# Writing two masked operands of a state-space scan over all 128 partitions

## The chip, the cores and the metric

The kernel runs on one core of one Trainium2 chip. The metric is the device time of one execution in microseconds (us), given as the median of several runs. A single profiled execution supplies the page and the trace from which the other numbers come. Its engines are called PE (TensorE, matrix products), DVE (VectorE), ACT (ScalarE), POOL (GpSimd) and SP (SyncE, which here only issues transfers).

## The reference

The reference is one block of a network on `x` of shape (4, 512, 256): four batch rows, 512 positions, 256 channels. It computes a modulated layer norm, a state-space attention (32 heads, head dimension 8, state size 64) added with a gate, a second modulated layer norm and a gated feed-forward layer with a Walsh-Hadamard transform, added with another gate. The part that matters here is the attention:

```python
xBC, z, A_log = jnp.split(proj, [CONV_DIM, CONV_DIM + D_INNER], axis=-1)
xc = lax.conv_general_dilated(xBC.transpose(0, 2, 1), conv_w, (1,), [(D_CONV - 1, 0)], ...)
x, Bm, Cm = jnp.split(xBC, [D_INNER, D_INNER + NH * D_STATE], axis=-1)
...
a = -jax.nn.softplus(A_log).transpose(0, 2, 1)
Lm = jnp.exp(segsum(a))
M = jnp.einsum('blhn,bshn,bhls->bhls', Cm, Bm, Lm)
y = jnp.einsum('bhls,bshp->blhp', M, x)
y = y + D[None, None, :, None] * x
out = (y * jax.nn.silu(z + z_bias)) @ W_out.T
```

Every head has a lower-triangular 512 x 512 matrix of decays, and `x` of that head (512 x 8) is multiplied by it.

## The kernel before, in words

The sequence is cut into 8 chunks of 64 positions (`Q`, `NC`). Within a chunk the kernel uses the quadratic form (`attend`, `intra`). Between chunks it carries states: `states` sums decayed `B` times `x` over each chunk, `turn_states` transposes those sums and runs a scan over the chunks on DVE, and `inter` multiplies `C` by the result.

The work is split in units `n = (i, b)`: half `i` of the heads (16 of them) and batch row `b`, eight in all. A unit has 8 steps `k`, one for each pair of heads (one partition half for each head of the pair). A step projects `B` and `C` with six PE matrix products each (`project`, `proj`, L242), applies a causal convolution of width 4 to each (`conv`: two ACT operations, two DVE operations at L378 and L379, one POOL operation at L380), transposes `B` (`turn_b`) and forms the masked products with the decays (`attend`; DVE at L446). Four steps make a group `m`; its parity is `pp`. `states`, `intra`, `turn_states` and `inter` run once for each `m`.

The change concerns `x_part3`, which runs once for each unit, and what it feeds. After the convolution of `x` (`x_proj`), `x_part2` makes two copies of each chunk side by side, so that a PE transpose of 128 columns yields the 64 positions of a chunk twice: on partitions 0 to 63 and again on 64 to 127. There are two such halves of a unit (`hf`), of four chunks each, and the transposed tile `pt` of a half is [128, 4 chunks, 128 channels] in PSUM. From it DVE makes two operands in SBUF:

- `xpad`, the weights of `intra`: for each `pp`, chunk and group `g`, 32 columns, of which the head of the lower partition half has its 8 columns filled on partitions 0 to 63 and the head of the upper half on 64 to 127. All else is zero, written once at the start by a POOL memset (L149). Four copies a half unit fill it (L506).
- `xwz`, the weights of `states`: `x` times the decay to the end of its chunk (`wdec`), with the even chunk of a pair on the lower partitions and the odd one on the upper, each in its own 16 of 32 columns, and zeros elsewhere from the same memset. Four products a half unit fill it (L514).

`wdec` is made once for each batch row in part 4 of `prologue`, by one ACT copy of a PE transpose (L366). `own` is a constant of ones and zeros loaded at the start. `own[p, 0, c]` is 1 where the partition half of `p` equals the half `c // 8` of the 16 columns; `turn_states` uses the whole of it to mask the states.

The order of work is set in two layers. The kernel pushes calls on an agenda with due times (`at_time`, and the table `T`), measured in steps `k`, and the program is traced in that order; unit `n`'s `x_part3` is due at 8n + 3.77, just ahead of `states` of its first group. A planner then orders the instructions on each engine when the program is built, by its own estimate of when each is ready, and gives the tiles their places in SBUF and PSUM. SP's transfers alone keep the order of tracing. PSUM tiles of the tag `m` (transposes, `pG`, `pl`, state sums, `pw`) share three buffers, and the projections (tag `p`) share three more.

After step 64 the kernel goes over to the feed-forward stage (`ffn_up`, `ffn_down`), of which the first pieces overlap the last steps of the scan.

Of the kernel before, what the change touches and what calls it, by code (L numbers as in the profile page):

```python
# [13 lines left out]
F32 = mybir.dt.float32  # L14
F32R = mybir.dt.float32r
BF16 = mybir.dt.bfloat16
AF = mybir.ActivationFunctionType
ALU = mybir.AluOpType
# [4 lines left out]
NH, HD = 32, 8  # L23
# [7 lines left out]
def mamba_ffn(tc, ctx, u, c_t, wmod, win_t, cw, cb, zb, dsk, wo_t, w13_t, w2_t,  # L31
              k_ident, k_reset, k_dl, k_dr, k_had, k_own, out):
    nc = tc.nc
    ve, ac, gp, pe = nc.vector, nc.scalar, nc.gpsimd, nc.tensor
# [4 lines left out]
    const = E(tc.tile_pool(name="const", bufs=1))  # L39
# [15 lines left out]
    def cload(src, shape, name, eng=nc.scalar):  # L55
        t = const.tile(shape, F32, name=name)
        eng.dma_start(t, src)
        return t
# [10 lines left out]
    def load_x(which, b, src, step=4):  # L69
        t = work([128, 4, DM], f"x{which}{b}", "x", 1)  # L70
        for n in range(0, 4, step):
            nc.sync.dma_start(t[:, n : n + step], src[:, n : n + step])
        return t

    def tok_rows(ap):
        return ap.rearrange("(t p) d -> p t d", p=128)
# [25 lines left out]
    ident = cload(k_ident, [128, 128], "ident", nc.sync)  # L102
# [41 lines left out]
    own = cload(k_own, [128, 4, 16], "own")  # L144
    xpad = const.tile([128, 2, NC, 4, 32], F32, name="xpad")
    sts = [const.tile([128, NC - 1, 4, 32], F32, name=f"sts{pp}") for pp in range(2)]
    xwz = const.tile([128, 4, 4, 2, 2, 16], F32, name="xwz")
    for t in (xpad, xwz):
        gp.memset(t, 0.0)  # L149

    dls = [const.tile([94, 8, 128], BF16, name=f"dl{n}") for n in range(2)]
    drs = [const.tile([94, 4, S], BF16, name=f"dr{n}") for n in range(2)]
# [110 lines left out]
    def normalize(b, which, x):  # L263
        mv = work([128, 4, 2], f"mv{which}{b}", "mv")
        rs = work([128, 4], f"rs{which}{b}", "rs")
        xn = work([128, 4, DM], f"xn{which}{b}", "xn", 1)
        for t in range(4):
            bs = work([128, 6], f"bs{which}{b}{t}", "bs")
            ve.bn_stats(bs, x[:, t])
            ve.bn_aggr(mv[:, t], bs)  # L270
        ve.tensor_scalar(rs, mv[:, :, 1], EPS, None, ALU.add)
        last[gp] = gp.tensor_tensor(rs, rs, neghalf, ALU.pow)
        for t in range(4):
            ve.tensor_scalar(xn[:, t], x[:, t], mv[:, t, 0:1], rs[:, t : t + 1], ALU.subtract, ALU.mult)
        return xn
# [19 lines left out]
    def spill(name, tiles):  # L295
        d = dram.tile([128, 2, 2, S], F32, name=name)
        for k in range(2):
            after(2, nc.sync.dma_start, d[:, k], tiles[k].bitcast(F32))
        return d
# [10 lines left out]
    wdec, p_dr, p_dr3, p_end = {}, {}, {}, {}  # L310
# [3 lines left out]
    def prologue(b, part, fill=None):  # L314
        if part == 0:
            if b not in x_in:
                x_in[b] = load_x(0, b, tok_rows(u[b]))
            xns[b] = normalize(b, 0, x_in.pop(b))
        elif part == 1:
            fulls[b], ht[0, b] = modulate(b, 0, xns.pop(b))  # L320
            htd[b] = spill(f"htd{b}", ht[0, b])
        elif part == 2:

            full = fulls.pop(b)
            pa = mtile([128, 128], f"pa{b}")
            for k in range(2):
                for t in range(4):
                    last[pe] = pe.matmul(pa[32 * t : 32 * t + 32], wa[:, k], full[k][:, 128 * t : 128 * t + 128],
                              start=(k == 0), stop=(k == 1), skip_group_check=True, tile_position=(0, 32 * t))
            e = work([128, 128], f"spe{b}", "spe", 1)  # L330
            at = work([128, 128], f"at{b}", "at", 1)
            ac.activation(e, pa, AF.Abs)
            last[ve] = ve.tensor_scalar(at, pa, 0.0, -1.0, ALU.max, ALU.mult)
            if fill:
                fill()
            ac.activation(e, e, AF.Exp, scale=-1.0)
            ac.activation(e, e, AF.Ln, bias=1.0)
            ve.tensor_tensor(at, at, e, ALU.subtract)
            phs = phss[b] = work([128, 128], f"phs{b}", "phs", 1)
            ve.tensor_tensor_scan(phs, reset, at, 0.0, ALU.mult, ALU.add)  # L340

            parts = work([128, 3, 128], f"parts{b}", "parts", 1, BF16)
            rest = work([128, 128], f"rest{b}", "at", 1)
            ve.tensor_copy(parts[:, 0], phs)
            ve.tensor_tensor(rest, phs, parts[:, 0], ALU.subtract)
            ve.tensor_copy(parts[:, 1], rest)
            last[ve] = ve.tensor_tensor(parts[:, 2], rest, parts[:, 1], ALU.subtract)
            p_dr3[b] = dram.tile([NH, 3, S], BF16, name=f"p3{b}")
            p_dr[b] = dram.tile([NH, S], F32, name=f"pd{b}")
            p_end[b] = dram.tile([NH, NC], F32, name=f"pend{b}")  # L350
            for t in range(4):
                (gp if T["p3gp"] and b == 0 and t % 2 else nc.sync).dma_start(p_dr3[b][:, :, 128 * t : 128 * t + 128], parts[32 * t : 32 * t + 32])
            after(1, write_sums, b, phs)
        elif part == 3:

            phs = phss.pop(b)
            df = dfs[b] = work([128, 128], f"df{b}", "df", 1)
            p_c = phs.rearrange("p (c l) -> p c l", l=Q)
            ve.tensor_tensor(df.rearrange("p (c l) -> p c l", l=Q), p_c[:, :, Q - 1 :].to_broadcast([128, 2, Q]),
                             p_c, ALU.subtract)  # L360
            ac.activation(df, df, AF.Exp)
        else:
            pw = mtile([128, 128], f"pw{b}")
            pe.transpose(pw, dfs.pop(b), ident)
            wdec[b] = const.tile([128, 4, NH], F32, name=f"wd{b}")
            ac.activation(wdec[b].rearrange("p t h -> p (t h)"), pw, AF.Copy)  # L366

    def write_sums(b, phs):
        for t in range(4):
# [126 lines left out]
    def x_part3(n):  # L496
        i, b = units[n]
        for hf, xd in enumerate(xds.pop(n)):
            pt = mtile([128, 4, 128], f"xt{n}{hf}")
            for c in range(4):  # L500
                pe.transpose(pt[:, c], xd[:, c].rearrange("p r l -> p (r l)"), ident)
            for pp in range(2):
                for j in range(2):
                    o = 8 * (2 * pp + j)
                    src = pt[64 * j : 64 * j + 64].rearrange("p c (g x) -> p c g x", g=4)[:, :, :, o : o + 8]
                    ve.tensor_copy(xpad[64 * j : 64 * j + 64, pp, 4 * hf : 4 * hf + 4, :, o : o + 8], src)  # L506
            for q in range(2):
                sl = slice(64 * q, 64 * q + 64)
                for t in range(2):
                    tt = 2 * hf + t  # L510
                    src = pt[sl, 2 * t + q].rearrange("p (a h x) -> p a h x", h=2, x=8)
                    dst = xwz[sl, tt, :, :, q].rearrange("p g a (h x) -> p (g a) h x", x=8)
                    wv = wdec[b][sl, tt, 16 * i : 16 * i + 16].rearrange("p (a h) -> p a h", h=2)
                    ve.tensor_tensor(dst, src, wv.unsqueeze(3).to_broadcast([64, 8, 2, 8]), ALU.mult)  # L514

    def states(m):
        pp = m % 2
        pst = mtile([128, 4, 128], f"ps{m}")
        for t in range(4):
            for g in range(4):  # L520
                pe.matmul(pst[32 * g : 32 * g + 32, t], xwz[:, t, g, pp].rearrange("p q x -> p (q x)"),
                          bts[4 * m + g][:, t], start=True, stop=True, tile_position=(0, 32 * g))
        for g in range(4):
            bts.pop(4 * m + g)
        stt[m] = work([128, 4, 128], f"st{m}", "st", 1)
        ac.activation(stt[m], pst, AF.Copy)
# [16 lines left out]
    def turn_states(m):  # L543
        n, pp = divmod(m, 2)
        st = stt.pop(m)
        pt = mtile([128, 4, 16, NC], f"sT{m}")
        for t in range(4):
            pe.transpose(pt[:, :, :, 2 * t : 2 * t + 2].rearrange("p g x q -> p g q x"), st[:, t], ident)
        sn = work([128, 4, 16, NC], f"sn{m}", "xd", 2)
        ve.tensor_tensor_scan(sn.rearrange("p g x c -> p (g x c)"),  # L550
                              dcs[n][:, 8 * pp : 8 * pp + 8].rearrange("p h x c -> p (h x c)"),
                              pt.rearrange("p g x c -> p (g x c)"), 0.0, ALU.mult, ALU.add)
        o = 16 * pp
        gp.tensor_tensor(sts[pp][:, :, :, o : o + 16].rearrange("p c g x -> p g x c"), sn[:, :, :, : NC - 1],
                         own.unsqueeze(3).to_broadcast([128, 4, 16, NC - 1]), ALU.mult)
# [323 lines left out]
```

## Time and profile before

| | us |
|---|---|
| median of 3 runs | 608.14 (607.9 to 608.25) |
| profiled execution, its own time | 611.31 |
| its span, first to last instruction | 609.4 |
| PE busy in the span | 549.5 |
| DVE busy | 454.3 |
| ACT busy | 367.5 |
| POOL busy | 314.9 |

The profiled execution is 3.2 us longer than the median, and 1.9 us of its own time lie outside the span. Its mean granted PE clock was 0.976. In the views that follow, a group is named by line, engine, operation, and output and input tiles; a wait is written "engine line <- engine line that released it: us in total, times, longest". Busy time of an engine is not a sum of durations where neighbours overlap: DVE reports the next operation of a run before the last one has ended.

### The profile page before, as it was taken

The page shows a single profiled execution, that of the slowest core. Times are in us where ns is not written, and L with a number is a line of the kernel's source. Part 1 is how long each engine was busy: PE and PEld are TensorE (multiplying, and loading weights), DVE is VectorE, ACT ScalarE, POOL GpSimd, SP SyncE. Part 2 cuts the span into 40 slices and gives each one's busy share as a digit, 9 for nine tenths or more (in the row PEclk, how much of TensorE's full clock was granted, in tenths as well). Part 3 has the DMA queues.
Part 4 walks back from the last instruction along what each step waited for, and adds up shares of the span by engine and source line. Part 5 has one row for each costly group of instructions (what it writes and reads, how often), then busy time and mean ns, then how long its engine had stood idle before and what let it go on. Part 6 is the DMA issues. An engine that isn't in the chain of part 4 may idle for free. (4 is left out here: it accounts for less than half of the span.)

```text
span 609.4 us, 16345 instructions
## 1 busy us (share of the span) xinstructions
PE 549.5 (90%) x6836; PEld 435.8 (72%) x6836; DVE 454.3 (75%) x820; ACT 367.5 (60%) x600; POOL 314.9 (52%) x288
## 2 busy tenths in 40 slices
PE   3777898899889979999999899979979999999996
PEld 3554676678667756676777576757857888888886
DVE  5978798897796879889879888989888384343342
ACT  5657678867867765697785678567643233322221
POOL 5564243644534476764655558456576545325341
PEclk9978999999889989999999999999988999999999
DMA  6331111020313305201501244145139033304021
GB/s 199 107 127 70 40 37 72 10 67 3 105 27 101 110 2 164 92 3 58 170 4 37 75 131 146 58 131 176 37 119 298 9 124 117 125 0 147 1 78 36
DMA packets 42113, 52.00 MB, mean 85 GB/s; under 512 B 18230, under 2 KB 30260, under 8 KB 42040
## 3 DMA queue, kind: packets, MB, share of 16 engines
q1 hardware_dynamic: 40504, 50.54, 26.2%
q8 instruction: 54, 0.88, 0.6%
q10 hardware_dynamic: 1472, 0.38, 0.3%
q14 instruction: 19, 0.16, 0.1%
q0 software_dynamic: 64, 0.05, 0.0%
HBM read 33.51 MB, written 17.44 MB: 84 GB/s over the span
## 5 line engine op out<-in xcount | busy, mean ns | idle before, releaser
L380 POOL TENSOR_TENSOR cc<-cc,cv 128x509 f32<-128x509 f32 x64 | 70.5, 1101 | 75.2 <-DVE cc L379 69.7
L380 POOL TENSOR_TENSOR bc<-bc,cv 128x509 f32<-128x509 f32 x64 | 71.3, 1114 | 58.0 <-DVE bc L379 34.5
L242 PE MATMUL f<-h,wf 128*128 128x512 f32 x384 | 98.3, 396 | 0.0
L242 PEld LDWEIGHTS f<-h,wf 128*128 128x128 f32 x384 | 69.4, 191 | 12.3
L694 POOL TENSOR_TENSOR fl<-ft,fh 128x512 fp32r<-128x512 f32 x31 | 40.1, 1294 | 64.1 <-ACT fh L693 60.7
L375 ACT ACTIVATE cc<-pcc,cb_sb,cw_sb 128x512 f32<-128x512 f32 x64 | 49.8, 778 | 26.5 <-PE pcc L242 15.0
L375 ACT ACTIVATE bc<-pbc,cb_sb,cw_sb 128x512 f32<-128x512 f32 x64 | 50.0, 781 | 24.7 <-PE pG L255 15.2
L242 PE MATMUL pcc<-ht,wq 128*128 128x512 f32 x192 | 55.7, 428 | 10.0 <-DVE bc L379 8.1
L378 DVE SCALAR_TENSOR_TENSOR cc<-pcc,cw_sb,cc 128x511 f32<-128x511 f32 x64 | 47.4, 741 | 20.9 <-ACT cv L377 19.9
L242 PE MATMUL pbc<-ht,wq 128*128 128x512 f32 x192 | 56.7, 432 | 5.5 <-DVE cc L379 4.0
L693 ACT ACTIVATE fh<-ft 128x512 fp32r<-128x512 f32 x32 | 20.2, 632 | 66.9 <-PE pdyi L701 36.8
L689 DVE SCALAR_TENSOR_TENSOR ft<-ft,f 128x512 f32<-128x512 f32 x32 | 21.9, 687 | 49.6 <-ACT ft L688 45.4
L242 PE MATMUL pcc<-hr,wq 128*128 128x512 f32 x192 | 52.1, 405 | 3.0 <-ACT cv L377 1.5
L242 PE MATMUL pbc<-hr,wq 128*128 128x512 f32 x192 | 51.7, 404 | 2.2 <-DVE cc L379 2.0
L242 PEld LDWEIGHTS pcc<-ht,wq 128*128 128x128 f32 x192 | 37.4, 202 | 20.4 <-DVE bc L379 4.1
L454 ACT ACTIVATE bt<-bT 128x512 f32<-128x512 f32 x64 | 38.6, 604 | 19.6 <-PE bT L452 19.5
L378 DVE SCALAR_TENSOR_TENSOR bc<-pbc,cw_sb,bc 128x511 f32<-128x511 f32 x64 | 47.3, 740 | 3.0 <-ACT cv L377 3.0
L242 PEld LDWEIGHTS pbc<-ht,wq 128*128 128x128 f32 x192 | 37.2, 203 | 17.3 <-DVE cc L379 1.9
L379 DVE SCALAR_TENSOR_TENSOR bc<-pbc,cw_sb,bc 128x510 f32<-128x510 f32 x64 | 47.4, 741 | 1.2
L379 DVE SCALAR_TENSOR_TENSOR cc<-pcc,cw_sb,cc 128x510 f32<-128x510 f32 x64 | 47.4, 741 | 1.1
L452 PE MATMUL bT<-ident,bc 128*128 128x128 f32 x256 | 41.8, 286 | 3.9 <-DVE cc L379 1.2
L377 ACT ACTIVATE cv<-pcc,cw_sb 128x512 f32<-128x512 f32 x64 | 43.7, 683 | 2.0 <-POOL bc L380 2.0
(148 smaller groups left out, 1237.0 us busy)
## 6 DMA issues: line engine op xcount, KB each, us to landing
wq<-win_t SPq DMA_DIRECT2D x16, 256.0 KB
htd<-ht SPq DMA_DIRECT2D x8, 512.0 KB
hr<-htd SPq DMA_DIRECT2D x8, 512.0 KB
h2d<-ht SPq DMA_DIRECT2D x8, 512.0 KB
h<-h2d SPq DMA_DIRECT2D x8, 512.0 KB
x<-u SPq DMA_DIRECT2D x7, 512.0 KB
ex<-pd SPq DMA_DIRECT2D x8, 256.0 KB
ygd<-yg SPq DMA_DIRECT2D x4, 512.0 KB
```

The costliest lines, as they stand in the source:

```text
L242: last[pe] = pe.matmul(ps, w[:, a, k, c0 : c0 + 128], ht[k][:, b], start=(n == 0), stop=(n == 5))
L375: ac.activation(dst, ps, AF.Identity, bias=cb_sb[:, tl : tl + 1], scale=w[:, 3:4])
L377: last[ac] = ac.activation(v, ps, AF.Copy, scale=w[:, 0:1])
L378: ve.scalar_tensor_tensor(dst[:, 1:], ps[:, : S - 1], w[:, 2:3], dst[:, 1:], ALU.mult, ALU.add)
L379: ve.scalar_tensor_tensor(dst[:, 2:], ps[:, : S - 2], w[:, 1:2], dst[:, 2:], ALU.mult, ALU.add)
L380: last[gp] = gp.tensor_tensor(dst[:, 3:], dst[:, 3:], v[:, : S - 3], ALU.add)
L452: pe.transpose(pt[:, t], bc[:, 128 * t : 128 * t + 128], ident)
L454: ac.activation(bts[k], pt, AF.Copy)
L689: ve.scalar_tensor_tensor(t, t, 1.0, p1, ALU.add, ALU.mult)
L693: ac.activation(hi, t, AF.Copy)
L694: (ve if (b, f) == (NB - 1, 7) else gp).tensor_tensor(lo, t, hi.bitcast(F32), ALU.subtract)
```

## The change

All operations that fill `xpad` and `xwz` now cover all 128 partitions, and the zeros come from masks instead of from partition slices and the memset. For `xpad`, one product of a half's `pt` with `own[:, 0]` writes both `pp` and all four groups; the view `v` addresses the 16 columns of each `pp` (0 to 15 and 16 to 31). For `xwz`, `wdec` gets an axis `q` for the even and the odd chunk of a pair, and is written by two ACT copies, each with a column of `own` as its scale, which zeroes the partition half that `q` doesn't own. One product for each pair of chunks then fills `xwz`. The layout of `xwz` goes from (group, pp, q, 16 columns) to (head, q, 8 columns), so `states` takes two heads at a time, and the transposes in `turn_states` write their columns in the order that puts the states back as before. `xwz` needs no memset.

```diff
-    xwz = const.tile([128, 4, 4, 2, 2, 16], F32, name="xwz")
-    for t in (xpad, xwz):
-        gp.memset(t, 0.0)
+    xwz = const.tile([128, 4, 16, 2, 8], F32, name="xwz")
+    gp.memset(xpad, 0.0)
...
-            wdec[b] = const.tile([128, 4, NH], F32, name=f"wd{b}")
-            ac.activation(wdec[b].rearrange("p t h -> p (t h)"), pw, AF.Copy)
+
+            wdec[b] = const.tile([128, 4, 2, NH], F32, name=f"wd{b}")
+            for q in range(2):
+                ac.activation(wdec[b][:, :, q], pw.rearrange("p (t h) -> p t h", h=NH), AF.Copy,
+                              scale=own[:, 0, 8 * q : 8 * q + 1])
...
-            for pp in range(2):
-                for j in range(2):
-                    o = 8 * (2 * pp + j)
-                    src = pt[64 * j : 64 * j + 64].rearrange("p c (g x) -> p c g x", g=4)[:, :, :, o : o + 8]
-                    ve.tensor_copy(xpad[64 * j : 64 * j + 64, pp, 4 * hf : 4 * hf + 4, :, o : o + 8], src)
-            for q in range(2):
-                sl = slice(64 * q, 64 * q + 64)
-                for t in range(2):
-                    tt = 2 * hf + t
-                    src = pt[sl, 2 * t + q].rearrange("p (a h x) -> p a h x", h=2, x=8)
-                    dst = xwz[sl, tt, :, :, q].rearrange("p g a (h x) -> p (g a) h x", x=8)
-                    wv = wdec[b][sl, tt, 16 * i : 16 * i + 16].rearrange("p (a h) -> p a h", h=2)
-                    ve.tensor_tensor(dst, src, wv.unsqueeze(3).to_broadcast([64, 8, 2, 8]), ALU.mult)
+
+            v = xpad[:, :, 4 * hf : 4 * hf + 4, :, :16].rearrange("p a c g x -> p a (c g) x")
+            v = bass.AP(v.tensor, v.offset, [v.ap[0], [v.ap[1][0] + 16, 2], *v.ap[2:]])
+            ve.tensor_tensor(v, pt.rearrange("p c (g a x) -> p a (c g) x", g=4, a=2),
+                             own[:, 0].unsqueeze(1).unsqueeze(1).to_broadcast([128, 2, 16, 16]), ALU.mult)
+            for t in range(2):
+                ve.tensor_tensor(xwz[:, 2 * hf + t].rearrange("p h q x -> p q h x"),
+                                 pt[:, 2 * t : 2 * t + 2].rearrange("p q (h x) -> p q h x", x=8),
+                                 wdec[b][:, 2 * hf + t, :, 16 * i : 16 * i + 16]
+                                 .unsqueeze(3).to_broadcast([128, 2, 16, 8]), ALU.mult)
...
-                pe.matmul(pst[32 * g : 32 * g + 32, t], xwz[:, t, g, pp].rearrange("p q x -> p (q x)"),
+                pe.matmul(pst[32 * g : 32 * g + 32, t], xwz[:, t, 4 * g + 2 * pp : 4 * g + 2 * pp + 2].rearrange("p h q x -> p (h q x)"),
...
-            pe.transpose(pt[:, :, :, 2 * t : 2 * t + 2].rearrange("p g x q -> p g q x"), st[:, t], ident)
+            pe.transpose(pt[:, :, :, 2 * t : 2 * t + 2].rearrange("p g (h x) q -> p (g h) q x", h=2), st[:, t], ident)
```

## The prediction

> **What bounds the kernel now.** I read the busy shares first, then a table by stage, then the places that the change touches, then who waits for whom.
>
> ```profile
> PE 549.5 (90%) x6836; PEld 435.8 (72%) x6836; DVE 454.3 (75%) x820; ACT 367.5 (60%) x600; POOL 314.9 (52%) x288
> ```
>
> The shares alone name TensorE (PE), but they average over stages. A table of busy time over four stretches (us; each engine's busy time with its instruction count, then clock and DMA) separates them:
>
> ```profile
> 0.00:65.00 65.00, 42.63 (x307) 32.08 (x307) 50.85 (x104) 42.97 (x65) 33.54 (x39) 0.92 0.38 120
> 65.00:470.00 405.00, 373.05 (x5698) 285.80 (x5699) 345.47 (x623) 285.52 (x472) 224.87 (x204) 0.98 0.27 84
> 480.00:610.00 130.00, 124.05 (x734) 109.93 (x733) 53.33 (x88) 36.07 (x60) 49.95 (x40) 0.99 0.23 74
> ```
>
> The third column is PE, the fifth is VectorE (DVE). After 480 us, in the feed-forward stage, PE works 124 of 130 us and DVE only 53: nothing that DVE saves counts there. All eight places of the change lie between 65.7 and 440.1 us, in the scan stage. There PE is busy 373.05 of 405 us, so 32 us of PE idle is all that a change off PE can win back, and DVE is busy 345 us (85%). The waits of PE in that stretch say who keeps it idle:
>
> ```profile
> PE sT L548 <- DVE l L446: 7.0, 4, 4.0
> PE pcc L242 <- DVE bc L379: 5.6, 5, 1.9
> PE pbc L242 <- DVE cc L379: 4.9, 4, 1.6
> PE pcc L242 <- ACT cv L377: 3.2, 2, 1.7
> PE ps L521 <- DVE xwz L514: 1.4, 4, 0.4
> ```
>
> Adding up every row of that answer, about 28 us of PE's waits end on DVE and 4 us on ACT. Few are on the tiles of the change itself (1.4 us on `xwz`): DVE is late with convolutions and products that queue behind other DVE work. The eight blocks of `x_part3` are such work. In windows of 8 us around each:
>
> ```profile
> 64.00:72.00 8.00, 6.25 (x115) 4.34 (x113) 7.76 (x22) 4.42 (x9) 2.18 (x2) 1.00 0.16 25
> 118.80:126.80 8.00, 7.46 (x123) 5.27 (x121) 7.73 (x23) 5.17 (x9) 2.89 (x3) 1.00 0.22 49
> 171.50:179.50 8.00, 6.53 (x112) 4.62 (x112) 7.73 (x23) 5.74 (x11) 1.09 (x1) 0.79 0.13 32
> 226.50:234.50 8.00, 7.43 (x122) 5.46 (x120) 7.76 (x23) 4.90 (x9) 3.45 (x3) 1.00 0.64 199
> 274.00:282.00 8.00, 7.20 (x123) 4.94 (x121) 7.73 (x23) 5.74 (x10) 3.16 (x3) 1.00 0.32 109
> 378.30:386.30 8.00, 8.00 (x137) 7.06 (x136) 7.77 (x22) 4.05 (x7) 2.90 (x3) 1.00 0.01 2
> ```
>
> DVE is full in every one (about 7.75 of 8). PE loses 1.75, 0.54, 1.47, 0.57 and 0.80 us in the first five, 5.1 us together, and nothing in the last three. The chain of waits can be followed back only to 328 us, and within it the two complete blocks lie on it from end to end (379.66 to 384.08 and 435.99 to 440.40).
>
> **What the Trainium skill says.** "VectorE: DVE Perf Modes", section "The TRN2 errata", gives (N+151)/0.96 ns for an fp32 product of two tensors of N elements a partition: 291 ns for 128 and 691 for 512, where this trace has 284 (L514) and 680 (L446). The same section says that many small tiles each pay the fixed part, which a large one pays once. Its section "Why PSUM operands drop a tier" lets no fp32 operation that reads PSUM run above one element a cycle, so replacing the PSUM copies by products loses no faster mode; the trace agrees, 287 ns a copy against 284 a product. "SBUF — State Buffer" is the last place: its section "Who interferes with whom" has VectorE and GpSimd share a port, with two-SBUF-input operations affected. The new products read one operand from PSUM, and the rows of that kind hold still here (L446 673 to 692 ns), while L338, with both operands in SBUF, takes 871 ns for 128 elements.
>
> **The change, part by part.**
>
> *Removed from DVE.* Per half unit four 64x128 copies (L506) and four 64x128 products (L514). One block on DVE:
>
> ```profile
> 379.58 1.21 DVE L506 COPY xpad<-xt 64x128 f32<-64x128 f32 x4
> 380.80 0.99 DVE L514 TENSOR_TENSOR xwz<-xt,wd 64x128 f32<-64x128 f32 x4
> 381.83 1.21 DVE L506 COPY xpad<-xt 64x128 f32<-64x128 f32 x4
> 383.05 1.00 DVE L514 TENSOR_TENSOR xwz<-xt,wd 64x128 f32<-64x128 f32 x4
> 384.08 0.75 DVE L379 SCALAR_TENSOR_TENSOR cc<-pcc,cw_sb,cc 128x510 f32<-128x510 f32 x1
> ```
>
> From 379.58 to 384.08 it holds DVE 4.50 us, 2.25 a half, 36.0 us over eight units.
>
> *Added to DVE.* Per half one 128x512 product of PSUM with a broadcast mask, and two of 128x256. For 512, L446 and L604 give 680 ns; a pair of L446 takes 1.28 us, so one step of a run is 0.60. For 256 no row of this kind exists: on the line between 284 (128) and 680 (512) it is 416 ns (424 by the page's formula), and between the steps 0.25 and 0.60 it is 0.37. A half is then 0.60 + 2 x 0.37 = 1.34 us, a unit 2.68: **relief of 1.82 us a unit, 14.6 us in all**. If nothing overlaps, a half is 0.68 + 2 x 0.42 = 1.52, and the relief 1.46 a unit, 11.7 in all. I take 1.82.
>
> *Added to ACT.* `wdec` takes two ACTIVATEs in place of one, four times: 4 x 278 ns (L366) = 1.1 us on an engine that is 60% busy. Its first reader comes at 66.9 us and the first L366 at 34.7; the later ones, up to 177.4, are likewise some 50 us ahead of theirs. The tile `pw` holds one of three shared PSUM buffers 0.28 us longer. I cost this at nothing; with its cover gone, 1.1 us.
>
> *Removed from POOL.* The memset of `xwz`, 952 ns at 2.50. POOL then sits idle 0.83 us until ACT's `th`, and the first PE work waits for a DMA until 8.07: nothing gained.
>
> *Moved in order.* The two layouts of `xwz` give the weights of `states` as 32 contiguous numbers either way. The transposes of `turn_states` write PSUM in runs of 8 instead of 16 at the same stride; L548 (strided, 285 ns) and L452 (dense, 286) cost the same, so I price that at nothing, with 0.1 us a unit on either side. No DMA is moved, and no queue is passed. The first product of a half serves both `pp` at once, so it must wait for the last `intra` of the unit before to have read `xpad`; those reads end some 20 us earlier (355.75 before the block at 379.58): no wait.
>
> *What reaches the end.* In the first five blocks the relief is larger than or about equal to PE's idle time, but part of that idle ends on ACT or on PE's own order: I take 60% of 5.1, **3.1 us**. In the other three PE has no gap; DVE merely comes out 1.8 us ahead, which shows at the next wait of PE on DVE, and PE does the same work in between: a third of 3 x 1.82, **1.8 us**. Sum 4.9 us. What is late next is PE itself and ACT's `cv` (18.4 us of DVE's own waits in the stage). The profiled execution took 611.31 us (span 609.4 and 1.9 around it), 3.2 above the median of the three runs; the gain is a difference, so I take it from the median: 608.14 - 4.9 = 603.2 us.
>
> **The rivals.**
>
> *Hidden.* PE is busy 92% of the stage and gap-free in three of the blocks, so DVE might gain slack that only becomes waiting for PE and ACT (59 us of DVE idle exist in the stage already). Against it: 28 us of PE's waits end on DVE. Time: 607 to 608.5.
>
> *The order shifts, slower.* Instruction order is fixed by a planner at build time, and it does react: at 67.91 us a convolution stands between the halves of the first block, at 381.8 nothing does. New durations, and 2 KB a partition more for `wdec`, may place other work differently. The mechanism with a price: `turn_states` needs one of the three shared PSUM buffers and finds it held by `pG` until DVE makes `l` (L446). That wait occurs four times now, 7.0 us, 1.75 each. Four more would cost 7.0, net of 4.9 a loss of 2.1: 610.2 us. It decides from three additional ones on (4.9/1.75 = 2.8). It is the case that ends on the other side.
>
> *More passes through.* If every block delays PE downstream, most of the relief counts: 8 to 11 us, 597 to 600; the ceiling is 14.6, so 593.5.
>
> *The products are dearer.* With three free dimensions and a doubly repeated operand they might run at half rate: 2 x 1.52 = 3.0 a half, 12 us more DVE work, a third of it on the path, 612 us. L514 already walks three free dimensions with a repeated operand at 284 ns, so this is unlikely, as is a splitting of the operations.
>
> **How the numbers follow.** The forecast (601 to 606.5) 0.45; more passes 0.17; hidden 0.12, of which a third is still over 0.2% faster; the shift 0.22; dearer products 0.04. Under 0.2%, 1.2 us, this kernel can't be told from no change. So faster 0.66, same 0.10, slower 0.24. The range 597 to 611 takes in half of the shift's cases and most of the larger gain; the likeliest case alone is 601 to 606.5.
>
> **What would show it.** In the changed profile: 16 products of `xpad` at 0.68 us and 32 of `xwz` at 0.42; DVE busy down by 11 to 15 us in all; a block of 2.7 us; eight ACTIVATEs of `wd` at 0.28; PE idle between 65 and 470 us down from 32 to about 27, with the FFN stage unchanged. The forecast is wrong if PE's waits on DVE don't fall, or if waits of `sT` on `l` grow.

## The result, and the profile after

The changed kernel takes 603.18 us in the median of 14 runs (599.66 to 606.49), against 608.08 for the kernel before in its 14 (606.44 to 610.71): a ratio of 0.9916, 95% interval 0.9891 to 0.994. It is 4.9 us faster, clear of the bound of 0.2%. The profiled execution took 605.11 us, with a span of 603.2.

The page of the changed kernel, busy time of each engine (share of the span) and instructions:

```profile
PE 544.0 (90%) x6836; PEld 435.3 (72%) x6836; DVE 438.3 (73%) x740; ACT 368.5 (61%) x604; POOL 313.3 (52%) x287
```

DVE has 80 instructions and 16.0 us less. PE keeps its 6836 products. One block on DVE, from its timeline (start, duration, engine, line, operation), now reads:

```profile
375.61 0.68 DVE L507 TENSOR_TENSOR xpad<-xt,own 128x512 f32<-128x512 f32 x1
376.21 0.74 DVE L510 TENSOR_TENSOR xwz<-xt,wd 128x256 f32<-128x256 f32 x2
376.87 0.68 DVE L507 TENSOR_TENSOR xpad<-xt,own 128x512 f32<-128x512 f32 x1
377.47 0.74 DVE L510 TENSOR_TENSOR xwz<-xt,wd 128x256 f32<-128x256 f32 x2
378.13 0.73 DVE L381 SCALAR_TENSOR_TENSOR cc<-pcc,cw_sb,cc 128x510 f32<-128x510 f32 x1
```

From 375.61 to 378.13 it holds DVE 2.52 us, where the old one held it 4.50. The rows by line give the single prices (engine, operation, count, then shortest, median and longest in ns):

```profile
L507 DVE TENSOR_TENSOR xpad<-xt,own x16: 677/679/681, 62.4 to 431.4; 128x512 f32<-128x512 f32 x16
L510 DVE TENSOR_TENSOR xwz<-xt,wd x32: 409/413/416, 63.6 to 432.4; 128x256 f32<-128x256 f32 x32
L367 ACT ACTIVATE wd<-pw,own x8: 361/368/422, 34.7 to 173.0; 128x128 f32<-128x128 f32 x8
```

The two products cost what was forecast. How many partitions take part hardly matters: the straight line through 413 and 679 ns, both on 128 partitions, gives 280 ns for 128 elements, and the old products on 64 partitions took 284. The `wdec` copies are dearer than the plain copy was.

So far all agrees. The waits of PE between 65 and 470 us do not; these are the largest rows (us in total, times, longest):

```profile
PE pbc L241 <- DVE cc L381: 5.2, 5, 1.6
PE pcc L241 <- DVE bc L381: 4.3, 6, 1.8
PE sT L547 <- DVE l L448: 4.2, 3, 1.9
PE ps L520 <- DVE l L448: 2.7, 2, 2.5
PE pt L283 <- DVE sn L549: 2.6, 2, 1.3
PE pl L418 <- DVE sn L549: 2.6, 2, 1.9
PE pbc L241 <- DVE bc L381: 2.5, 1, 2.5
```

All rows together, 27.6 us still end on DVE, and it was 28. `sT` waits less, as do `pcc` and `xwz`; but `ps`, `pt`, `pl` and `pbc` have waits that were smaller before or absent. A gain that leaves the suspected waits as large as they were isn't explained by them. Nor does the pair of profiles show where PE saved its time: the span is 6.2 us shorter, but PE's idle time in it only fell from 59.9 to 59.2 us. The other 5.5 us are busy time of the same 6836 products, at a mean granted clock of 0.976 and 0.980; what shortened it isn't shown. The planner had put many instructions in another order, on PE and DVE above all, so two things changed at once: the work and the order.

### The profile page after: what moved, and what is told of

The parts are those of the page before. It is cut to its first block, busy times and chain, and to the rows that moved or that the text cites. A ratio compares the mean times of both kernels' runs of the same rounds, so it can differ in the third digit from the quotient of the medians.

```text
span 603.2 us, 16262 instructions
## 1 busy us (share of the span) xinstructions
PE 544.0 (90%) x6836; PEld 435.3 (72%) x6836; DVE 438.3 (73%) x740; ACT 368.5 (61%) x604; POOL 313.3 (52%) x287
## 4 chain that ended last, share of the span: by engine, by line
PE 61%; DVE 19%; DMA 8%; ACT 7%; issue 3%; SPq 2%; POOL 1%; ACTq 0%; DVEq 0%; POOLq 0%
PE f L241 14%; PE pcc L241 9%; PE pbc L241 9%; PE pdy L700 4%; PE pdyi L700 4%; PE py L536 3%; PE bT L454 3%; PE pG L254 3%; PE ps L520 3%; DVE cc L380 2%; PE po L600 2%; DMA wq<-win_t 2%; PE pz L241 2%; DVE l L448 2%; DMA x<-u 2%
## 5 line engine op out<-in xcount | busy, mean ns | idle before, releaser
L377 ACT ACTIVATE bc<-pbc,cb_sb,cw_sb 128x512 f32<-128x512 f32 x64 | 49.9, 780 | 35.0 <-PE pG L254 18.4
L377 ACT ACTIVATE cc<-pcc,cb_sb,cw_sb 128x512 f32<-128x512 f32 x64 | 49.8, 778 | 23.2 <-PE pcc L241 13.7
L241 PEld LDWEIGHTS pbc<-hr,wq 128*128 128x128 f32 x192 | 34.9, 191 | 13.1 <-issue 1.9
```

Source lines behind the costliest of these rows:

```text
L241: last[pe] = pe.matmul(ps, w[:, a, k, c0 : c0 + 128], ht[k][:, b], start=(n == 0), stop=(n == 5))
L377: ac.activation(dst, ps, AF.Identity, bias=cb_sb[:, tl : tl + 1], scale=w[:, 3:4])
```

## The experiments

**Work and order apart.** The planned order of a kernel can be kept while its operations are exchanged: behind the last call on the agenda, each engine's instructions are chained one behind the other, by index in the order of tracing (`ORDER`, not printed here, holds these indices as start:length). Such a chain is meant to fix the order of issue and to add no wait for completion. In the traces DVE's 692 operations other than those on `xpad` and `xwz` come in one sequence in every kernel with the old order and in another in every kernel with the new one, with some 50 of them moved. Where the planner puts the tiles is not held fixed.

```diff
         now[0], _, fn, args = heappop(agenda)
         fn(*args)
+    keep_order(tc, nc)
+
+def keep_order(tc, nc):
+    traced = list(nc.cur_bb.bb.instructions)
+    info = mybir.DependencyInfo(mybir.DependencyClass.NoSync, mybir.DependencyReason.DATA)
+    for text in ORDER.values():
+        before = None
+        for run in text.split(","):
+            a, _, n = run.partition(":")
+            for k in range(int(a), int(a) + int(n or 1)):
+                if before is not None:
+                    tc.add_manual_dep(traced[k], before.name, info, reason="keep_order")
+                before = traced[k]
```

With two kinds of work and two orders there are four kernels. "Old" is that of the kernel before. The runs were spread over several chips; every ratio is to runs of the kernel before on the same chip, so across the experiments the ratios are compared.

*Old work, old order.*

> The kernel before, with every engine's instructions pinned to the order that the planner had given it: a control for the pinning itself. Both theories expect the time of the kernel before, 608 us within 1.2 us.

Measured: 609.11 us, ratio 1.0007 (0.9989 to 1.0024). Pinning itself costs nothing that shows.

*New work, old order.*

> The three masked products a half unit, with every engine pinned to the order of the kernel before (a product stands where the last of the operations stood that it replaces). Theory 'less DVE work': the gain is there in full, about 603 us, and every block of x_part3 hands its 1.8 us on. Theory 'another order': the lead of 3.3 us that the changed kernel has already at its first block is the planner's, so with the old order most of the gain is gone, 606 to 608 us.

Measured: 599.78 us, ratio 0.9849 (0.981 to 0.9888). The gain is not only there, it is nearly twice the 4.9 us of the change as it was made: 9.3 us against the control, more than either theory expected. The granted clock is not the reason: its mean is 0.981 in these six executions and in the 36 of the kernel before beside them.

*Old work, new order.*

> The eight operations a half unit of the kernel before, with every engine pinned to the order that the planner gave the changed kernel. Theory 'less DVE work': as slow as the kernel before, 607 to 609 us. Theory 'another order': 603 to 605 us, the gain without any saving of work.

Measured: 612.6 us, ratio 1.0062 (1.0037 to 1.0087). The new order is no gain; alone it costs some 3 us, which neither theory expected.

*New work, new order.*

> The changed kernel with every engine pinned to its own planned order, the second control. Both theories expect the time of the changed kernel, 603 us within 1.2 us.

Measured: 600.93 us, ratio 0.9877 (0.9838 to 0.9916), a little better than expected. A second comparison of the unpinned kernel was to tell whether pinning helps:

> The changed kernel as it is, once more beside the kernel before on this chip. With its order pinned it measured 0.988 of before, unpinned 0.992 in the comparison of the change. If the difference is only the spread of chips and runs, it comes between the two, 0.987 to 0.992; if pinning an order changes which waits are placed and that pays, it stays at 0.991 to 0.993.

Measured: 603.43 us, ratio 0.9891 (0.9862 to 0.992), inside the expected band: spread, with no sign of an effect of pinning. The two orders with the new work were then set side by side once more:

> The changed operations with the order of the kernel before, once more, to set against the next run on the same chip. Theory 'the new order costs something': 0.985 of before, 2 to 3 us ahead of the next run. Theory 'the two orders are equal and the chips spread': within 1 us of it.

> The changed operations pinned to their own planned order, once more. Theory 'the new order costs something': 0.988 to 0.990 of before. Theory 'equal': the ratio of the run before this one, within 0.0017.

Measured: 598.65 us, ratio 0.9829 (0.9802 to 0.9856), and 602.65 us, ratio 0.9898 (0.9865 to 0.9932). The intervals are apart: with the new work, too, the new order is the worse, by 4.0 us here. In the first pair it was 1.2 us, with intervals that overlap. The work, in turn, counts as much in the new order as in the old: it takes the ratio there from 1.0062 to between 0.9877 and 0.9916 (four comparisons), which is 9 to 11 us.

The trace shows where the order counts. These are the windows from the first block's start to the last one's (stretch, its length, then busy us of PE, PE's weight loads, DVE, ACT and POOL with counts), for the kernel before, the changed one, the old work in the old order, and the new work in the old order:

```profile
65.66:435.91 370.25, 343.38 (x5219) 262.23 (x5220) 313.53 (x562) 270.86 (x449) 204.63 (x188) 0.99 0.25 76
```

```profile
62.36:430.16 367.80, 340.73 (x5219) 262.87 (x5220) 300.74 (x492) 272.84 (x454) 204.39 (x188) 0.99 0.25 77
```

```profile
63.42:433.50 370.08, 341.81 (x5219) 261.25 (x5220) 313.19 (x562) 270.97 (x449) 204.59 (x188) 0.99 0.25 76
```

```profile
64.68:425.68 361.00, 339.47 (x5219) 260.84 (x5220) 298.69 (x492) 271.89 (x452) 204.32 (x188) 0.99 0.25 78
```

All four hold the same 5219 PE products. In one and the same order the new work shortens this stretch from 370.08 to 361.00 us, and PE idle in it (length less busy) from 28.3 to 21.5. The other 2.3 us lie in PE's busy time, for which I have no explanation. In the planner's new order it lasts 367.80, with 27.1 us of PE idle; over all profiles of the new work it is 363.0 to 367.8 us in the new order (four) and 361.0 and 361.1 in the old. With the old work the new order makes it 375.8 us. The new order has one merit: the first block starts at 60.9 to 62.4 us in the five profiles that have it, at 63.2 to 66.5 in the eight with the old order. That is the lead of about 3 us which I had taken for the gain of the order before the experiments; the scan gives it back, and in most profiles more.

PE's waits in the new work with the old order, between 65 and 470 us:

```profile
PE pcc L241 <- DVE bc L381: 6.2, 6, 2.3
PE sT L547 <- DVE l L448: 4.9, 3, 2.7
PE pbc L241 <- DVE cc L381: 4.8, 5, 1.4
...
PE ps L520 <- DVE l L448: 1.3, 2, 1.1
PE pt L283 <- DVE sn L549: 1.2, 1, 1.2
PE pl L418 <- DVE sn L549: 1.2, 2, 0.7
```

Against the changed kernel, `ps`, `pt` and `pl` are 1.4 us smaller each and the wait of `pbc` on `bc` (2.5) is gone; `pcc` and `sT` are 2.6 larger together. Over all rows 23.9 us end on DVE (21.6 in the second profile of this kernel) instead of 27.6. With the new work these four rows hold the price of the new order. With the old work it is others: there `pcc` on `bc` grows from 4.3 to 7.4 us between the two orders and `ps` from 1.1 to 2.6, while neither `pt` nor `pbc` on `bc` waits. So what in the new order costs the time stays open; nothing was moved alone in an experiment.

**How much DVE time is worth.** Three more kernels keep the order of the kernel before and change the length of the block. The first two do one half of the change.

```diff
 # xpad only: the kernel before, with
-            for pp in range(2):
-                for j in range(2):
...
-                    ve.tensor_copy(xpad[64 * j : 64 * j + 64, pp, 4 * hf : 4 * hf + 4, :, o : o + 8], src)
+            v = xpad[:, :, 4 * hf : 4 * hf + 4, :, :16].rearrange("p a c g x -> p a (c g) x")
...
+            ve.tensor_tensor(v, pt.rearrange("p c (g a x) -> p a (c g) x", g=4, a=2), ...
 # xwz only: the changed kernel, with the opposite replacement
```

> Only xpad is written by a masked product; xwz keeps its four products a half unit, its layout, its memset and the single copy of wdec. All engines pinned to the order of the kernel before. A half goes from 1.21 + 1.04 us to 0.60 + 1.04, 0.6 us less, 9.8 us of DVE over 16 halves. Theory 'DVE time, whichever operation it comes from': about two thirds of that, as with both parts (9.3 of 14.6 us), so 601 to 603 us. Theory 'it matters that xpad comes sooner, since PE's intra is next in line': nearly the whole gain of both, 599 to 600.

Measured: 601.61 us, ratio 0.9865 (0.983 to 0.9901); the block holds DVE 3.25 us.

> Only xwz is written by two masked products with the doubled wdec; xpad keeps its four copies a half unit. All engines pinned to the order of the kernel before. A half saves 1.0 - 0.66 us, some 0.3 to 0.4, 5 to 6 us of DVE over 16 halves. Theory 'DVE time': 3 to 4 us faster than before, 604 to 605 us. Theory 'xpad sooner': within 1.2 us of before.

Measured: 603.41 us, ratio 0.9908 (0.9879 to 0.9937); the block holds DVE 3.78 us. By the ratios each part alone gives more than I had expected of it, 8.2 and 5.6 us, and `xwz`, at which `xpad` comes no sooner, gives its share. Their sum, 13.8 us, is more than the two give together (9.2 and 10.4 by the two ratios): the second part is worth less once the first is there.

The third keeps the new operations but makes the block long again:

```diff
-            ve.tensor_tensor(v, pt.rearrange(...), own[:, 0]..., ALU.mult)
-            for t in range(2):
+            for _ in range(2):
+                ve.tensor_tensor(v, pt.rearrange(...), own[:, 0]..., ALU.mult)
+            for t in (0, 1, 1):
```

> The changed operations with the order of the kernel before, but xpad's product is issued twice and the second product of xwz too, so that a half holds DVE 2 x 0.60 + 3 x 0.33 = 2.2 us, as long as the eight old operations (2.25). Theory 'DVE time': the gain is gone, 607 to 609 us. Theory 'fewer operations and waits, or earlier readiness of the operands': most of the gain stays, 600 to 603 us.

Its block on DVE:

```profile
380.62 1.41 DVE L508 TENSOR_TENSOR xpad<-xt,own 128x512 f32<-128x512 f32 x2
381.94 1.20 DVE L511 TENSOR_TENSOR xwz<-xt,wd 128x256 f32<-128x256 f32 x3
383.06 1.41 DVE L508 TENSOR_TENSOR xpad<-xt,own 128x512 f32<-128x512 f32 x2
384.38 1.21 DVE L511 TENSOR_TENSOR xwz<-xt,wd 128x256 f32<-128x256 f32 x3
385.50 0.74 DVE L381 SCALAR_TENSOR_TENSOR cc<-pcc,cw_sb,cc 128x510 f32<-128x510 f32 x1
```

It holds DVE 4.88 us, a little longer than the old one, in ten operations instead of sixteen. Measured: 612.17 us, ratio 1.005 (1.0033 to 1.0067). The whole gain is gone. It was the time on DVE, and neither the number of operations nor the masks. An earlier readiness of the operands is not ruled out by this run, since the repeated products finish them late as well; but in the kernel before PE's products waited only 1.4 us for `xwz` and not at all for `xpad`, so little of 9.3 us can come from there.

The last one takes the block away in units 1 to 7:

```diff
             for c in range(4):
                 pe.transpose(pt[:, c], xd[:, c].rearrange("p r l -> p (r l)"), ident)
+            if n:
+                continue
```

> An upper bound: the order of the kernel before, and only the first unit writes xpad and xwz, so that units 1 to 7 compute with the operands of unit 0 (that part of the computation is left out). DVE has 31.5 us less than in the kernel before (7 x 4.50), 17 us less than with the new products. Theory 'the gain goes with DVE time': two thirds again, 588 us. Theory 'DVE time counts until PE is the bound': the first 15 us gave 9 to 10; the next 17 give less than half of that rate, 593 to 597 us.

Measured: 600.36 us, ratio 0.9857 (0.9831 to 0.9883). That is no faster than with the new products. Together, all in the order of the kernel before, with the length of the seventh unit's block:

| kernel | DVE held by one block, us | ratio to the kernel before |
|---|---|---|
| new products, repeated | 4.88 | 1.0050 |
| old operations | 4.51 | 1.0007 |
| `xwz` by products | 3.78 | 0.9908 |
| `xpad` by products | 3.25 | 0.9865 |
| both | 2.52 | 0.9849, 0.9829 |
| none in units 1 to 7 | 0 | 0.9857 |

From 4.88 to 3.25 us a block, 13.0 us of DVE over eight units, the time falls by 0.0185 of 608, 11.2 us: **0.86 us for each us of DVE**. The next 0.73 us a block (5.8 us in all) bring 1 to 2 us, and the remaining 2.52 (17.6 us over seven units) nothing.

The chains of waits (followed back from the last instruction, at each step to what released it) agree with that. With the repeated products 23.5 us of the chain lie on blocks, on six of the eight; with `xwz` by products 14.3 us on four; with `xpad` by products 6.0 us on two; with both 2.3 us on one, in each of the two profiles. With the old operations the last two blocks are all that can be seen, and the chain runs through both. These are the chains at the seventh block with the repeated products (380.6 to 385.6 us) and with the new ones (370.8 to 373.4), as shares of the window, where a piece that reaches over its edge counts whole:

```profile
by line: DVE xpad L508 52.0%; DVE xwz L511 36.2%; DVE cc L381 14.8%; DVE cc L380 13.2%; issue 7.8%
```

```profile
by line: PE pcc L241 56.8%; PE po L600 35.1%; PE py L536 22.5%
```

As the blocks get shorter the chain leaves them for PE, and what is left of them then costs nothing. What holds PE in the last kernel is this (65 to 470 us):

```profile
PE pbc L241 <- DVE cc L381: 4.4, 5, 1.7
PE sT L549 <- DVE l L448: 3.9, 3, 1.7
PE pcc L241 <- ACT cv L379: 3.7, 2, 2.0
PE pcc L241 <- DVE bc L381: 3.6, 4, 1.8
PE pl L418 <- DVE dx L479: 2.6, 2, 2.0
```

The waits that still end on DVE sum to 22.8 us, about what they were with the blocks in place (23.9 and 21.6 in the two profiles); those on ACT are 4.7 (2.4 and 3.8). The row's name for a releaser doesn't mean that more speed of that engine would help: DVE's own input then comes late. Ahead of `cc` alone DVE waits 19.7 us for ACT's `cv` with the new products, and without blocks

```profile
DVE cc L380 <- ACT cv L379: 26.7, 25, 2.2
```

Of the chain between 65 and 470 us, 233 us then lie on PE, 90 on DVE and 28 on ACT. That this ring of PE, ACT and DVE sets the floor, with PE the largest part, is my reading of the waits and the chain; no experiment shortened ACT or PE.

## Why the prediction was right, and where its steps were not

The forecast was 603.2 us, and 603.18 were measured. The sign, the price of the operations and the cause (less DVE time in a stage where PE waits for DVE) hold. But two steps were off and largely cancelled, so the closeness of the number is luck: the work gives 9.3 us where 4.9 were reckoned, and the order, reckoned at nothing, takes about 3 of them back.

- **The price of the products: right.** 680 and 416 ns were forecast, 679 and 413 measured. The step in a run was 0.33 us for the smaller one instead of 0.37, so the relief was 1.98 us a block and not 1.82; DVE fell by 16.0 us, just above the forecast 11 to 15.
- **The skill's formula: right here, beyond what it is stated for.** "VectorE: DVE Perf Modes" gives it in "The TRN2 errata" for additions of 512 and 2048 elements, in a section on operations that read SBUF. For these products, which read PSUM, (N+151)/0.96 gives 424 ns for 256 elements and 413 were measured. The section's remark that one large tile pays the fixed part once is what the relief consists of: eight operations of 128 elements and three of 512, 256 and 256 carry the same 1024 elements a partition. "Why PSUM operands drop a tier" holds as well: the trace shows no loss from turning PSUM copies into products.
- **Readings that don't matter to the sum.** The 871 ns of L338 are the mean of four operations that took 292 to 1362 ns, and of the eight windows the last has DVE busy for 7.33 of 8 us, not 7.75.
- **"What reaches the end": too small by half.** I had taken 60% of the PE idle inside the 8 us windows and a third of the relief in the gap-free blocks, 4.9 us. The true term, in an unchanged order, is 9.3 us. Idle time of PE inside a window does not bound what a saving on DVE brings: PE had no gap in three windows, yet a DVE that is ahead pays back at waits further on, which the profile also showed (28 us of them). The chain that ran through two whole blocks from end to end was the better guide: the measured rate is 0.86 us for each us until the block is down to about 3 us, where the chain leaves most of the blocks.
- **The shifted order: real, and beside the gain instead of in its place.** I gave it a chance of 0.22 as the case that ends slower. It happened: it costs 3 us with the old work (1.0062 against 1.0007) and between 1.2 and 4.0 with the new one. Its mechanism was not the one I named: the waits of `sT` on `l` fell, from 7.0 to 4.2 us with the new work and from 7.2 to 5.3 with the old. Which it is stays open, as the rows that grow differ between the two kinds of work. At its true size it lies below the 9.3 us, so the sign stayed.
- **More passes through.** This rival, 8 to 11 us, is what the work alone does.
- **The ceiling was too high.** 14.6 us, the whole relief, can't be had: the gain ends at about 10 us, as the kernel with blocks in the first unit alone shows.
- **The ACT copies: mispriced, and still without effect.** 368 ns each and not 278; eight of them less four old ones are 1.8 us and not 1.1. No row waits for `wd`.
- **Two signs that I had named failed.** PE idle between 65 and 470 us was to fall from 32 to 27; it is 33.1 (405 less 371.94). And PE's waits on DVE, whose failing to fall was to show the forecast wrong, went from 28.0 to 27.6 us, hardly a fall. They were bad signs, since they can't tell work from order: between the same blocks PE idle is 27.1 us against 26.9 before, and where the order was kept it fell from 28.3 to 21.5, the waits on DVE from 28.7 to 23.9.

## What to carry to other kernels

When a planner orders the instructions, an edit of the work is two edits, and a comparison of the two kernels measures their sum: keep the order and exchange the work, then keep the work and exchange the order. How much of a saving on a side engine counts is read from whether the chain of waits passes through its work, not from the idle time of the main engine beside it; and it counts until the chain has left that work, so the chain is read again after each step. The best version here is the new work in the old order, 598.65 to 599.78 us, faster than both kernels that were compared.

## What was not expected of the hardware

An ACT copy of 128x128 from PSUM takes 278 ns with a constant scale and 368 with a scale read from SBUF for each partition (the second also writes its output in pieces of 32); I had priced both alike. The trace of the kernel before held most of this price: its copies of 128x512 from PSUM take 604 ns without such a scale (L454) and 683 to 692 with one (L377). The doubly repeated mask and three free dimensions cost DVE nothing: 679 ns for 128x512, as for L446 with plain operands (680). Nor does a factor that is repeated eight times in a row: 413 ns for the 256 elements of `xwz`, where the line between 284 and 680 gives 416.
